# Neighbour masks from ScalarE's bfloat16 copy, and one diagonal add per graph, in a four-layer graph network

## The chip, the cores and the metric

One Trainium2 chip, one of its NeuronCores. The core has TensorE (PE: matmuls and transposes), VectorE (DVE), ScalarE (ACT), GpSimd (POOL) and DMA queues issued by SyncE (SP). The metric is the device time of one execution in microseconds (us); lower is better. Every time here is from runs of the kernel before or from the profile of one such execution.

## What is computed

There are 16 graphs of 1024 nodes with 64 channels, an adjacency matrix of zeros and ones per graph (self-loops included), and four residual layers with normalisation. Layer 0 thins the adjacency and then takes, for each node and channel, a weighted sum of the 25, 50 and 75 % quantiles over the remaining neighbours. Layers 1 to 3 are ordinary graph convolutions with the unthinned adjacency. The change lies in the thinning ("dilation"), whose reference is:

```python
adj_ = jnp.where(eye[None], 1.0, adj)
nb = (adj_ > 0) & (~eye)[None]               # neighbours without the node itself
m = nb.sum(-1)
rank = jnp.cumsum(nb, axis=-1) - 1
skip = jnp.where(m > 10, (m + 1) // 2, 1)
do_dil = (skip > 1) & mask
removed = nb & do_dil[..., None] & ((rank + 1) % skip[..., None] == 0)
rem = removed | jnp.swapaxes(removed, 1, 2)  # removed from either side
return jnp.where(rem, 0.0, adj_)
```

Layer 3 divides by the row sums of the adjacency (plus one), and those row sums are taken in the same pass over the matrix as the dilation.

## The kernel before, in words

**The main loop.** Layer 0 is done by counting. Each graph takes 96 slots (`SLOTS`, L1046), and the loop at L1365 walks 16 x 96 = 1536 slots. In each slot DVE makes one mask (`masks`, L636: tile `mt` from `cc` and `rB`, 128 x 2048) and one product (`products`, L644: tile `pr` from `mt` and `dw`, 128 x 4096). PE multiplies and ACT moves results out of PSUM for several earlier slots (`words` L654, `ranks` L666, `steps` L674) and for the counts of later units (`counts`, L596). A slot has two halves, and a half is called a place.

**Background work.** Between these the loop sets generators, each a piece of other work that is cut into steps by its `yield`s: `sort_pair` with `ranks_of` (L316, L263: the sort of the channel values of two graphs on DVE), `dilate` (L415: the dilation of the next graph), `degrees` (L788: column sums on ACT) and `layers` (L830: the rest of the network for the graph before). `Spread` (L977) decides at every place which generator may take a step. A generator gets a number of steps, a first and a last place, and a step is due when its share of the places has passed (`late`, L1038). A digit that is yielded is a least distance in places to the step before; a `p` marks a step with PE work in the one PSUM bank `ps_l`, of which one is taken per place; `h` holds that bank. `dilate(g + 1)` is given 64 steps over 168 of the graph's 192 places (L1381). The sort is a filler (L1017): it steps where the planner's sum of DVE time (`Ordered.count`, L185) isn't too far ahead of its sum of PE time.

**Order.** While `Ordered.on` holds, each PE, DVE and ACT instruction is linked to the one before it on its engine (`link`, L137), so every engine runs its instructions in just the order in which the Python code issued them. An instruction that waits keeps all behind it on its engine waiting.

**The dilation** works on eight blocks of 128 rows (t = 0 to 7) of the matrix of one graph:

- L422 `block_of` loads a block as two halves `da` of 128 x 512 in float32. There are two such buffers; the loads of block t + 1 are issued right after the readers of block t.
- L435 to L439: for each half, DVE compares (`is_gt` 0) from `da` to the float16 neighbour mask `nb`, and ACT copies `da` to `q`, the block's row of the result tile `vt`, adding up the rows as it goes (`accum_out`). The copy itself is never read.
- L442: DVE clears the diagonal block of `nb` (`offdiag`); L444: DVE scans `nb` to the running count `cum`. `nb` and `cum` are the halves of tile `sc`, of which there is one.
- L451 to L456: POOL works out the row's skip from the last count; L459: ACT overwrites `q` with the distance |cum + bias|, in two halves.
- L464: DVE turns `q` to 1 (removed) or 0.25 (kept). Then two late steps: `edges` (L466) multiplies by `nb`, and `own` (L469) adds 0.25 on the diagonal block, `later` (L205) lets them out one by one after a mask or a product.

When all eight blocks are done, PE transposes pairs of blocks (L484), and DVE combines each with its mirror image (L487, L495), which leaves 1 for an edge that neither side removed.

The dilation of graph 0 runs ahead of the main loop, one step beside each step of the first sort (L1083 to L1100); those of graphs 1 to 15 run beside the main loop of the graph before.

Of the kernel before, what the change touches and what calls it, by code (L numbers as in the profile page):

```python
# [10 lines left out]
F16 = mybir.dt.float16  # L11
BF16 = mybir.dt.bfloat16
# [3 lines left out]
AF = mybir.ActivationFunctionType  # L16
ALU = mybir.AluOpType
AX = mybir.AxisListType

P = 128  # L20
# [22 lines left out]
def gnn_stack(  # L43
# [22 lines left out]
    B, N, C = x.shape  # L66
    H = W1.shape[1]
    L = gW.shape[0]
    T = N // P
    HALF = N // 2  # L70
    V = nc.vector

    const = ctx.enter_context(tc.tile_pool(name="const", bufs=1))
# [27 lines left out]
    ident = const.tile([P, P], F32, name="ident")  # L101
    make_identity(nc, ident)
    ident16 = const.tile([P, P], F16, name="ident16")
    V.tensor_copy(ident16, ident)
    offdiag = const.tile([P, P], F16, name="offdiag")
    V.tensor_scalar(offdiag, ident, -1.0, 1.0, ALU.mult, ALU.add)
    one16 = const.tile([P, 2], F16, name="one16")
    V.memset(one16, 1.0)

# [9 lines left out]
    for i in range(2):  # L119
        t = const.tile([P, N], F16, name=f"prow{i}")  # L120
# [76 lines left out]
    V, A = Ordered(nc.vector, "DVE"), Ordered(nc.scalar, "ACT")  # L197
# [7 lines left out]
    def later(*calls):  # L205

        item = list(calls)
        waiting.append(item)
        return item
# [205 lines left out]
    def dilate(g, found):  # L415

        mk = small.tile([P, T], F32, tag="mk", name="mk")
        V.tensor_copy(mk, mask8[:, g, :])
        den = small.tile([P, 2, T], F32, tag="den", name="den", bufs=3)
        vt = graph.tile([P, T, N], F16, tag="vt", name="vt", bufs=2)  # L420

        def block_of(t):  # L422
            a = []
            for h in range(2):
                a.append(strm.tile([P, HALF], F32, tag="da", name="da", bufs=2))
                nc.sync.dma_start(out=a[h], in_=adj[g, ts(t, P), ts(h, HALF)])
            return a

        a = block_of(0)
        yield  # L430
        for t in range(T):
            sc = dil.tile([P, 2 * N], F16, tag="d", name="sc")
            nb, cum = sc[:, 0:N], sc[:, N : 2 * N]
            q = vt[:, t, :]
            for h in range(2):  # L435
                V.tensor_scalar(nb[:, ts(h, HALF)], a[h], 0.0, None, ALU.is_gt)
                A.activation(
                    q[:, ts(h, HALF)], a[h], AF.Copy, accum_out=den[:, h, t : t + 1]
                )  # L439
            if t + 1 < T:  # L440
                a = block_of(t + 1)
            V.tensor_tensor(nb[:, ts(t, P)], nb[:, ts(t, P)], offdiag, ALU.mult)  # L442

            V.tensor_tensor_scan(cum, nb, nb, 0.0, ALU.add, ALU.max)  # L444
            yield
            m = cum[:, N - 1 : N]


            sk = small.tile([P, 5], F32, tag="sk", name="sk")
            G = nc.gpsimd  # L450
            G.tensor_scalar(sk[:, 0:1], m, 0.5, 0.5, ALU.add, ALU.mult)  # L451
            G.tensor_scalar(sk[:, 0:1], sk[:, 0:1], MAGIC, -MAGIC, ALU.add, ALU.add)
            G.tensor_scalar(sk[:, 1:2], m, T_THRESH, mk[:, t : t + 1], ALU.is_gt, ALU.mult)
            G.tensor_scalar(sk[:, 2:3], sk[:, 0:1], 1.0, sk[:, 1:2], ALU.add, ALU.mult)
            G.tensor_scalar(sk[:, 3:4], sk[:, 2:3], -1.5, 1.5, ALU.mult, ALU.add)
            G.tensor_scalar(sk[:, 4:5], sk[:, 2:3], 0.5, -0.5, ALU.mult, ALU.add)  # L456
            yield "5"

            for h in range(2):  # L459
                A.activation(  # L460
                    q[:, ts(h, HALF)], cum[:, ts(h, HALF)], AF.Abs, bias=sk[:, 3:4]
                )
                yield "2"
            V.tensor_scalar(q, q, sk[:, 4:5], 0.25, ALU.is_equal, ALU.max)  # L464

            def edges(q=q, nb=nb):  # L466
                V.tensor_tensor(q, q, nb, ALU.mult)

            def own(q=q[:, ts(t, P)]):  # L469
                V.scalar_tensor_tensor(q, ident16, 0.25, q, ALU.mult, ALU.add)  # L470

            rest = later(edges, own)
            yield "1"
            finish(rest)
        yield

        tiles = vt.rearrange("p j (t m) -> p j t m", m=P)
        for j in range(T):
            for t0 in range(j + 1, T, 4):
                yield PEV  # L480
                n = min(4, T - t0)
                pq = bank(ps_l, "pq", dt=F16).rearrange("p (i t m) -> p i t m", i=2, m=P)
                for i in range(n):
                    transpose(pq[:, 0, i], tiles[:, t0 + i, j], ident16)  # L484
                    transpose(pq[:, 1, i], tiles[:, j, t0 + i], ident16)
                for i, side in enumerate((tiles[:, j, t0 : t0 + n], tiles[:, t0 : t0 + n, j])):
                    V.scalar_tensor_tensor(  # L487
                        side, pq[:, i, 0:n], 0.25, side, ALU.is_equal, ALU.is_gt
                    )
        yield PEV  # L490
        pq = bank(ps_l, "pq", dt=F16).rearrange("p (t m) -> p t m", m=P)
        for j in range(T):
            transpose(pq[:, j], tiles[:, j, j], ident16)
        side = bass.AP(vt.tensor, vt.offset, [list(vt.ap[0]), [N + P, T], [1, P]])
        V.scalar_tensor_tensor(side, pq, 0.25, side, ALU.is_equal, ALU.is_gt)  # L495
        yield

        rd = dram.tile([S, N], F16, name="rd")
        rn = dram.tile([S, N], F16, name="rn")
        wd = dram.tile([S, N], F16, name="wd", bufs=3)  # L500
        yield PEV
        pm = bank(ps_l, "pm")
        for t in range(T):
            for j in range(T):
                matmul(
                    pm[:, t : t + 1], lhsT=vt[:, j, ts(t, P)], rhs=one16[:, 0:1],
                    start=(j == 0), stop=(j == T - 1), skip_group_check=True,
                )

        def wide_of(i):  # L510
            return by_s[:, i].unsqueeze(1).to_broadcast([P, T, S])

        pos = small.tile([P, T, S], F32, tag="pos", name="pos", bufs=1)
        nb1 = small.tile([P, T], F32, tag="nb1", name="nb1", bufs=1)
        rw = small.tile([P, T, 3 * S], F16, tag="rw", name="rw", bufs=1)
        r, w = rw[:, :, 0:S], rw[:, :, S : 2 * S]
        V.tensor_scalar(nb1, pm[:, 0:T], -1.0, 0.0, ALU.add, ALU.max)
        V.tensor_tensor(pos, nb1.unsqueeze(2).to_broadcast([P, T, S]), wide_of(0), ALU.mult)
        V.tensor_scalar(r, pos, 1023.625, 1024.0, ALU.add, ALU.max)
        V.scalar_tensor_tensor(pos, pos, 1024.0, r, ALU.add, ALU.subtract)  # L520
        V.tensor_tensor(w, pos, wide_of(1), ALU.mult)
        V.tensor_tensor(w, w, wide_of(2), ALU.add)
        V.scalar_tensor_tensor(pos, pos, 0.0, wide_of(3), ALU.is_gt, ALU.mult)
        V.tensor_tensor(r, r, pos, ALU.add)
        V.tensor_scalar(rw[:, :, 2 * S : 3 * S], r, 1.0, None, ALU.add)
        yield "4" + PEN
        pq = bank(ps_l, "pq", dt=F16)
        for t in range(T):
            transpose(pq[0 : 3 * S, ts(t, P)], rw[:, t], ident16)
        sc = dil.tile([P, 2 * N], F16, tag="d", name="sc")  # L530
        A.copy(sc[0 : 3 * S, 0:N], pq[0 : 3 * S])
        nc.sync.dma_start(out=rd, in_=sc[0:S, 0:N])
        nc.sync.dma_start(out=wd, in_=sc[S : 2 * S, 0:N])
        nc.sync.dma_start(out=rn, in_=sc[2 * S : 3 * S, 0:N])
        found.append((vt, rd, rn, wd, den))
# [511 lines left out]
    sorted_, parts, infos = [], [], {}  # L1047
# [189 lines left out]
    for i in range(2):  # L1237
        t = const.tile([P, N], F16, name=f"ranks{i}")
# [125 lines left out]
    pairs_of, background, resident = {}, [], ()  # L1364
    for y in range(n_units * S + S + 2):  # L1365
# [4 lines left out]
        if running and z == 0:  # L1370
            infos[g]["aggd"] = dram.tile([G8, P, HALF], F32, name="aggd")
            deg = small.tile([P, 3, T], F32, tag="deg", name="deg")
            base = 2 * SLOTS * g
            if g == 0 and TURN < B:
                background.append(
                    Spread(
                        sort_of(1, sorted_), 2 * n_sort + 11, 0, base + 2 * SLOTS + ROWS, True
                    )
                )
            if g + 1 < B:  # L1380
                background.append(Spread(dilate(g + 1, parts), 64, base, base + 168))  # L1381
            background.append(
                Spread(degrees(g, deg), 2 * T + 2, base, base + 184)
            )
            infos[g]["deg"] = deg
# [119 lines left out]
```

## Time and profile before

| What | Value |
|---|---|
| median of 3 runs | 8277.14 us (8274.99 to 8284.68) |
| the profiled execution's own time | 8271.02 us |
| its span in the trace | 8269.2 us |
| mean granted TensorE clock | 0.984 |
| first product of the main loop starts | 297.84 us |
| last product starts | 8129.1 us |
| busy DVE, PE, ACT, POOL | 7826.2, 7311.8, 7060.5, 1321.6 us |

All instructions that go through the ordering helper carry the helper's line, L176 (matmuls L156, transposes L152), so groups are told apart by their tiles: `sc<-da` is the compare, `vt<-da` ACT's copy with the row sums, `sc<-sc,offdiag` the clearing of the diagonal, `vt<-vt,sc` the step `edges`, `vt<-ident,vt` the step `own`. A form such as 128x512 f16<-128x512 f32 gives partitions x elements and type of output and input. The start of an instruction and the start of the next one on its engine lie closer together than its listed duration wherever the two may overlap.

### The profile page before, as it was taken

What the parts mean: (1) busy time and instruction counts of PE and PEld (TensorE: products, weight loads), DVE (VectorE), ACT (ScalarE), POOL (GpSimd) and SP (SyncE); (2) the same over time, 40 slices, a digit from 0 to 9 for tenths busy, and PEclk for the clock granted to TensorE, in tenths of its full rate; (3) what the DMA queues carried; (4) which work ended last, traced back from release to release, by engine and by line L of the source; (5) the groups of instructions that cost most, each with busy time, mean ns of one, the idle gap of its engine ahead of it and who ended that gap; (6) DMA issues with size and microseconds to landing.
All of it is one profiled execution on the core that took longest, in us unless ns stands there. A gap on an engine that the chain in (4) does not pass through costs nothing. (4 is left out here: it accounts for less than half of the span.)

```text
span 8269.2 us, 164242 instructions
## 1 busy us (share of the span) xinstructions
PE 7311.8 (88%) x65169; PEld 2994.8 (36%) x65169; DVE 7826.2 (95%) x8924; ACT 7060.5 (85%) x13562; POOL 1321.6 (16%) x942
## 2 busy tenths in 40 slices
PE   0688889999999899898899999999899999999997
PEld 0233333333333333333333333333333333334333
DVE  9899999999999999999999999999999999887874
ACT  1689889888898889989898898988989888899993
POOL 2210202112021110202112021210202112020000
PEclk9999999999999999999999999999999999999999
DMA  3212222232223232232233322233222233222222
GB/s 101 48 42 53 94 88 93 79 101 98 88 86 87 86 104 91 90 93 90 80 99 104 81 93 89 80 100 94 91 94 85 85 97 104 72 89 72 65 88 68
DMA packets 530453, 711.85 MB, mean 86 GB/s; under 512 B 201488, under 2 KB 328848, under 8 KB 529680
## 3 DMA queue, kind: packets, MB, share of 16 engines
q1 hardware_dynamic: 529680, 701.34, 27.3%
q8 instruction: 510, 8.36, 0.4%
q14 instruction: 263, 2.15, 0.1%
HBM read 602.38 MB, written 98.77 MB: 85 GB/s over the span
## 5 line engine op out<-in xcount | busy, mean ns | idle before, releaser
L176 DVE TENSOR_TENSOR pr<-mt,dw 128x4096 f16<-128x4096 f16 x1536 | 3507.8, 2284 | 222.7 <-PE pw L156 166.7
L156 PE MATMUL x<-vt,xw 128*128 128x512 f16 x8192 | 2317.9, 386 | 0.0
L176 DVE TENSOR_TENSOR mt<-cc,rB 128x2048 f16<-128x2048 f16 x1536 | 1864.7, 1214 | 15.4 <-ACT cc L176 15.4
L176 ACT ACTIVATE pv<-pv,col 128x512 f32<-128x512 f32 x1536 | 1077.1, 701 | 0.0
L156 PEld LDWEIGHTS <-xw 128*128 128x128 f16 x8192 | 737.8, 99 | 819.9 <-issue 298.3
L176 ACT ACTIVATE qq<-pw 128x512 f16<-128x512 f32 x1536 | 962.1, 626 | 16.5 <-PE pw L156 15.9
L156 PE MATMUL pv<-mt,txw 128*32 128x512 f16 x12288 | 951.6, 387 | 8.6 <-ACT pv L176 8.6
L176 ACT ACTIVATE val<-pv 128x512 f32<-128x512 f32 x1536 | 948.9, 618 | 9.2 <-PE pv L156 8.9
L156 PE MATMUL pw<-pr,red 128*32 128x512 f16 x12288 | 937.7, 381 | 14.7 <-DVE pr L176 14.7
L176 ACT ACTIVATE pa<-pa,col 128x512 f32<-128x512 f32 x1020 | 712.5, 699 | 224.8 <-PE pa L156 223.2
L176 ACT ACTIVATE dw<-y 128x512 f16<-128x512 f32 x1024 | 636.9, 622 | 261.2 <-PE y L156 238.7
L734 POOL TENSOR_TENSOR rstd<-var,neghalf 128x8 f32<-128x8 f32 x112 | 250.0, 2232 | 3473.9 <-DVE var L176 3473.9
L176 ACT ACTIVATE cc<-x 128x512 f16<-128x512 f32 x1024 | 620.9, 606 | 190.2 <-PE x L156 112.8
L176 ACT ACTIVATE xw<-pa,col 128x512 f16<-128x512 f32 x1020 | 700.8, 687 | 33.0
L176 ACT ACTIVATE dw<-y,col 128x512 f16<-128x512 f32 x1024 | 719.2, 702 | 1.6 <-PE pv L156 1.1
L156 PE MATMUL pw<-ranks,subr 128*32 128x512 f16 x6144 | 603.0, 382 | 66.5 <-ACT xw L176 64.1
L176 ACT ACTIVATE h<-x 128x512 f16<-128x512 f32 x1024 | 640.0, 625 | 1.0 <-PE x L156 1.0
L176 ACT ACTIVATE l<-x 128x512 f16<-128x512 f32 x1024 | 604.0, 590 | 9.4 <-PE x L156 9.2
L156 PE MATMUL pv<-qq,lead 128*32 128x512 f16 x6144 | 603.6, 381 | 0.0
L156 PE MATMUL x<-h,neg 128*128 128x512 f16 x1024 | 393.9, 385 | 225.3 <-ACT h L176 206.4
L156 PEld LDWEIGHTS <-txw 128*32 128x32 f16 x12288 | 186.3, 94 | 1051.0 <-issue 1050.3
L176 DVE TENSOR_TENSOR sr<-sr 128x384 f16<-128x384 f16 (+9 forms) x1328 | 546.4, 441 | 17.7
(226 smaller groups left out, 10547.6 us busy)
## 6 DMA issues: line engine op xcount, KB each, us to landing
a<-adj_dram SPq DMA_DIRECT2D x360, 512.0 KB
a<-adjT_dram SPq DMA_DIRECT2D x240, 512.0 KB
da<-adj_dram SPq DMA_DIRECT2D x256, 256.0 KB
ac<-adjT_dram SPq DMA_DIRECT2D x256, 256.0 KB
aggd<-v SPq DMA_DIRECT2D x128, 256.0 KB
rB<-rn SPq DMA_DIRECT2D x96, 256.0 KB
v<-aggd SPq DMA_DIRECT2D x192, 128.0 KB
w<-wd SPq DMA_DIRECT2D x96, 128.0 KB
```

The costliest lines, as they stand in the source:

```text
L156: link("PE", nc.tensor.matmul(out, **kw))
L176: ins = call(*args, **kw)
L734: nc.gpsimd.tensor_tensor(rstd, var, neghalf, ALU.pow)
```

## The change

The compare no longer reads the float32 block. ACT's copy is written in bfloat16 (the same bytes of `q`, read as another type), and one compare over 1024 elements reads that copy. It is put behind a new `yield "2"`, so at least two places after ACT's instructions were issued. The step `own` is gone; in its place one add per graph, over the eight diagonal blocks together, of a new constant `quarter` (0.25 on the diagonal). The dilation's share of the schedule goes from 64 to 72 steps over the same 168 places. The view `diag`, the same as the former `side`, is made earlier.

```diff
+    quarter = const.tile([P, P], F16, name="quarter")
+    V.tensor_scalar(quarter, ident, 0.25, None, ALU.mult)
...
             q = vt[:, t, :]
+            near = q.bitcast(BF16)
             for h in range(2):
-                V.tensor_scalar(nb[:, ts(h, HALF)], a[h], 0.0, None, ALU.is_gt)
                 A.activation(
-                    q[:, ts(h, HALF)], a[h], AF.Copy, accum_out=den[:, h, t : t + 1]
+                    near[:, ts(h, HALF)], a[h], AF.Copy, accum_out=den[:, h, t : t + 1]
                 )
             if t + 1 < T:
                 a = block_of(t + 1)
+            yield "2"
+            V.tensor_scalar(nb, near, 0.0, None, ALU.is_gt)
             V.tensor_tensor(nb[:, ts(t, P)], nb[:, ts(t, P)], offdiag, ALU.mult)
...
-            def own(q=q[:, ts(t, P)]):
-                V.scalar_tensor_tensor(q, ident16, 0.25, q, ALU.mult, ALU.add)
-
-            rest = later(edges, own)
+            rest = later(edges)
             yield "1"
             finish(rest)
         yield
 
         tiles = vt.rearrange("p j (t m) -> p j t m", m=P)
+        diag = bass.AP(vt.tensor, vt.offset, [list(vt.ap[0]), [N + P, T], [1, P]])
+        V.tensor_tensor(diag, diag, quarter.unsqueeze(1).to_broadcast([P, T, P]), ALU.add)
...
-        side = bass.AP(vt.tensor, vt.offset, [list(vt.ap[0]), [N + P, T], [1, P]])
-        V.scalar_tensor_tensor(side, pq, 0.25, side, ALU.is_equal, ALU.is_gt)
+        V.scalar_tensor_tensor(diag, pq, 0.25, diag, ALU.is_equal, ALU.is_gt)
...
-                background.append(Spread(dilate(g + 1, parts), 64, base, base + 168))
+                background.append(Spread(dilate(g + 1, parts), 72, base, base + 168))
```

## The prediction

> **What bounds the kernel now.** I read the page's busy table first. DVE has the largest share, but an average doesn't say where it counts, so next come the stretches of the span: one of the main loop (3280 to 3480), a leaner one just before it, and the last two graphs.
>
> ```profile
> PE 7311.8 (88%) x65169; PEld 2994.8 (36%) x65169; DVE 7826.2 (95%) x8924; ACT 7060.5 (85%) x13562; POOL 1321.6 (16%) x942
> ```
> ```profile
> core 0: us, PE busy (x) PEld busy (x) DVE busy (x) ACT busy (x) POOL busy (x), PEclk, DMA share, GB/s
> 0.00:150.00 150.00, 9.58 (x76) 6.04 (x77) 143.78 (x300) 36.64 (x93) 44.04 (x98) 1.00 0.31 99
> 150.00:200.00 50.00, 2.55 (x66) 2.19 (x63) 42.78 (x117) 1.20 (x2) 0.00 (x0) 1.00 0.40 111
> ...
> 3160.00:3240.00 80.00, 78.62 (x722) 32.48 (x721) 77.36 (x95) 67.68 (x128) 3.26 (x2) 1.00 0.37 124
> 3280.00:3480.00 200.00, 180.85 (x1615) 72.15 (x1613) 199.42 (x215) 187.07 (x367) 55.16 (x37) 1.00 0.28 93
> ...
> 7200.00:7680.00 480.00, 452.69 (x4118) 184.93 (x4116) 404.40 (x334) 444.77 (x857) 85.62 (x55) 1.00 0.24 79
> ```
>
> In 3280 to 3480 DVE is busy 199.42 of 200 us while PE and ACT have room: DVE's own work is the time there, and that is where the dilation's blocks lie. In 3160 to 3240 PE (78.62 of 80) is as full as DVE (77.36). From 7200 on, where the last dilation runs (its last compare starts at 7454.7), no sort is left, DVE idles 76 of 480 us, and a DVE instruction less is worth nothing. The same stretches for the products alone give the price of a slot: 195 products per 1000 us in the middle, 5.13 us each; 98 in 7200 to 7680, 4.90 us each. So without the sort a graph with a dilation beside it still takes 96 x 4.90 = 470 us against 492. What DVE saves counts fully until a graph has lost some 22 us; then PE and ACT are late next.
>
> The waits of DVE inside the loop agree: between 400 and 8000 us it waits 148.3 us in 133 pieces for PE (`pw`), 125.1 us of it after 7080, where the sort has ended, and never for the dilation's data.
>
> **The compare.** The groups by form give durations, the timeline gives what an instruction really takes of the queue, start to next start:
>
> ```profile
> L176 DVE TENSOR_SCALAR sc<-da 128x512 f16<-128x512 f32 x256 | 96.2, 416 | 0.0
> L176 DVE TENSOR_TENSOR vt<-vt,sc 128x1024 f16<-128x1024 f16 x128 | 87.3, 682 | 0.3
> L176 DVE SCALAR_TENSOR_TENSOR vt<-ident,vt 128x128 f16<-128x128 f16 x128 | 36.0, 281 | 0.0
> L176 DVE SCALAR_TENSOR_TENSOR vt<-pq,vt 128x1024 f16<-128x1024 f16 x16 | 19.5, 1216 | 0.0
> L176 DVE TENSOR_SCALAR sb<-sb 128x1024 f16<-128x1024 f16 x16 | 6.8, 426 | 0.5
> ```
> ```profile
> 3308.92 0.28 DVE L176 SCALAR_TENSOR_TENSOR vt<-ident,vt 128x128 f16<-128x128 f16 x1
> 3309.12 0.75 DVE L176 TENSOR_SCALAR sc<-da 128x512 f16<-128x512 f32 x2
> 3309.79 0.21 DVE L176 TENSOR_TENSOR sc<-sc,offdiag 128x128 f16<-128x128 f16 x1
> 3310.04 2.29 DVE L176 TENSOR_TENSOR_SCAN sc<-sc 128x1024 f16<-128x1024 f16 x1
> ...
> 3341.36 0.69 DVE L176 TENSOR_TENSOR vt<-vt,sc 128x1024 f16<-128x1024 f16 x1
> 3341.97 2.28 DVE L176 TENSOR_TENSOR pr<-mt,dw 128x4096 f16<-128x4096 f16 x1
> 3411.13 0.76 DVE L176 TENSOR_SCALAR sc<-da 128x512 f16<-128x512 f32 x2
> 3411.93 0.23 DVE L176 TENSOR_TENSOR sc<-sc,offdiag 128x128 f16<-128x128 f16 x1
> ```
>
> The pair of compares holds the queue 0.67 us (3309.12 to 3309.79) where the diagonal block lies in the first half, 0.80 (3411.13 to 3411.93) where it lies in the second; mean 0.735. The new compare is one TENSOR_SCALAR of 1024 two-byte elements. The trace has no bfloat16 source, so I bound it: 0.43 from `sb<-sb` (float16, same shape and operation class), 1.22 from the 128x1024 `vt<-pq,vt`, the slowest per element. I take 0.43, the row that differs in nothing but the kind of 16-bit number. The diagonal step depends on it and starts 0.03 after its end, as the scan does here (3309.79 + 0.21 to 3310.04), so 0.46. Saved: 0.735 - 0.46 = 0.275 us per block.
>
> **The diagonal.** `own` has a duration of 0.28 but the next instruction starts 0.20 after it (3308.92 to 3309.12). Eight of these go, 1.60 us per graph. One add of 8 x 128 float16 elements comes. Contiguous, that is `vt<-vt,sc`: 0.69, with the next start after 0.61 (3341.36 to 3341.97). The new one hops between eight blocks and repeats its second operand; `mt<-cc,rB` repeats an operand too and takes 1214 ns for 2048 elements, the same pace. Upper bound 1.22 (`vt<-pq,vt`); I take 0.61.
>
> Per graph: 8 x (0.275 + 0.20) - 0.61 = 3.19 us. Durations alone would say 8 x (752 - 426 + 281) - 682 = 4.17 us, since overlap is counted twice.
>
> Here the Trainium skill speaks for the smaller sum: "Vector Engine (DVE) Microarchitecture Reference", section "Measured stream behaviour on trn2", puts an instruction's fixed cost at about 75 ns once the queue overlaps, so that dropping or merging instructions frees little; "VectorE: DVE Perf Modes" gives about 150 cycles for one by itself, by which the sum would be the larger one. The trace's 0.20 for a 0.28 instruction sides with the first. [...]
>
> **Where it counts.** Dilations of graphs 1 to 14 run beside graphs 0 to 13, where DVE is the bound: 14 x 3.19 = 44.7 us. That of graph 15 runs in the idle of 7200 to 7680: 0. That of graph 0 runs beside the first sort, DVE busy 143.78 of 150: 3.2 us. The setup's extra `quarter` is hidden: the first sort step waits 0.71 us for its data behind the two conversions of `ident`; at worst 4.4 us (`offdiag`, same form, first of its kind).
>
> **What is moved.** The instruction order of the built programs shows eight more steps of graph 0's dilation moving past the end of the sort, among the rank steps, where DVE is idle 7.2 of 50 us (150 to 200) for loads of `m`. Bounds 0 to 7 us; I take 2. In the loop the blocks' compares move from slots 3, 10, 17, 24, 30, 37, 43, 50 to 3, 12, 19, 26, 33, 40, 47, 54, the transposes' combinations from slots 58 to 73 to 62 to 75, the row that hands ranks on from 80 to 76, all inside the 84 at which the next graph takes them; SP's loads of `da` move along, each still a whole block ahead and now freed by ACT alone. The sort, as filler, shifts too: in odd graphs the last 32 slots get 70 instead of 62 sort instructions, the first 24 get 22 instead of 32. The late slots are the lean stretch where PE bounds and DVE had 2.6 us idle in 80. Filling it is a gain of at most that, 7 x 2.6 = 18 us, but crowding slots 24 to 31 (34 instead of 24) could lose as much. I take +4.
>
> **The new wait.** The compare now waits for ACT. Behind it on DVE stand the diagonal step, the 2.29 us scan, and every mask and product; PE waits for those. Before, DVE's compare started between 2.1 us before and 6.0 us after the end of ACT's two copies, median 2.7 over the 128 blocks, -0.6 at worst up to graph 14. Two places are one slot, 5.13 us, so the least margin is about 4.5 us. A row with just this shape exists: `vt<-vt,sk` stands two places behind ACT's second half and waited 0.1 us in all of 128. I price it at 0. If that cover is gone, ACT's two copies with their sum reads take 1.3 us (3305.08 to 3306.40), so 1 us or more per block. ACT's writing of bfloat16 instead of float16 keeps its 0.66 us; between its quickest and slowest 128x512 form (0.59 and 0.70 us) it's off the path, as ACT has 13 us idle in 200. PE's transposes now follow the diagonal add by one to two slots, as they followed `own`; PE's 7.8 us of waiting for `vt` per 1000 us stays.
>
> **Sum:** 44.7 + 3.2 + 2 + 4 = 54 us. The profiled execution took 8271.0 (span 8269.2 plus 1.8), so 8217; the median shown is 6 us above it, so 8277 - 54 = **8223 us**.
>
> **Rivals.**
> - *Larger gain:* the full durations are freed (15 x 4.17 = 63) and the lean stretch fills (+12): 8277 - 75 = 8202. Against it stand the overlapping starts.
> - *Half pace:* a bfloat16 source gets the pace of 16-bit two-operand work, 0.68 as in `vt<-vt,sc`: 15 x 8 x 0.256 = 31 less, 8254. For it: no bfloat16 row.
> - *The planner eats it:* the reshuffled sort leaves PE-bound slots lean and DVE-bound slots crowded, so each graph loses its 3 us again: 8277, within 15. For it: in 3160 to 3240 PE is already full.
> - *Unpacked compare, slower:* the bfloat16 source runs at the pace of `vt<-pq,vt`, 1.22. Place: the 120 compares that count. Price: 1.22 - 0.43 = 0.79 each, 95 us, so 8277 - 54 + 95 = 8318. It turns the sign from a compare of 0.88 us on (54 / 120 = 0.45 above 0.43). Against: the casts in this trace from float32 and int32 to float16 take 0.69 for 1024, below that.
> - *The wait, slower:* ACT lags over 5 us behind; 1 us per block in 14 graphs is 112, 8335; it turns the sign at 0.48 us per block.
>
> **Numbers.** Forecast (8208 to 8240) 0.64; larger gain 0.08; half pace 0.07; planner 0.13; unpacked 0.04; wait 0.04. Changes under 0.2% (16.5 us) are about what can't be told from none. Faster: 0.64 + 0.08 + 0.07 = 0.79; same 0.13; slower 0.08. The range 8200 to 8262 holds the forecast, most of the larger gain, half pace and the planner's better edge, about 0.81.
>
> **What would show it.** In the new profile: a group `sc<-vt` 128x1024 x128 near 426 ns with no idle before it (half pace: 680; unpacked: 1200); no `vt<-ident,vt`; 16 adds `vt<-vt,quarter` near 690; DVE busy down by some 55 us; the middle at 5.10 us per product and 7200 to 7680 unchanged. Idle before `sc<-vt` put down to ACT would prove the wait; more idle of `pr` for PE in mid-loop would prove the planner.

## The result, and the profile after

| Kernel | Median (us) | Lowest to highest | Ratio to before, 95% interval |
|---|---|---|---|
| before | 8277.53 (4 runs) | 8274.99 to 8284.68 | 1 |
| after | 8340.97 (4 runs) | 8332.95 to 8344.41 | 1.0073 [1.0061, 1.0085] |

The changed kernel is 63 us slower; the forecast was 54 us faster, and the time lies outside the range of 8200 to 8262. The profiled execution of after has a span of 8342.3 us (before 8269.2), at a mean granted clock of 0.980 (before 0.984).

First the busy table of after, then the same two stretches as before.

```profile
PE 7344.7 (88%) x65169; PEld 2987.7 (36%) x65169; DVE 7777.7 (93%) x8685; ACT 7083.4 (85%) x13562; POOL 1238.2 (15%) x942
```
```profile
3280.00:3480.00 200.00, 184.22 (x1648) 74.12 (x1645) 195.89 (x197) 190.54 (x372) 46.25 (x32) 0.99 0.24 79
7200.00:7680.00 480.00, 455.25 (x4117) 185.31 (x4118) 399.60 (x318) 444.68 (x855) 79.29 (x55) 1.00 0.25 82
```

DVE has 239 instructions and 48.5 us of work fewer (7826.2 to 7777.7), as was wanted. But the span less DVE's busy time was 443.0 us and is now 564.6: DVE stands idle 121.6 us longer, and 121.6 - 48.5 = 73 is the difference of the two spans. In 3280 to 3480, where DVE had been busy 199.42 of 200 us, it is busy 195.89. The question is what it waits for.

These are the changed instructions in the groups by form of after (count, busy time and mean ns, then idle time just before them):

```profile
L178 DVE TENSOR_SCALAR sc<-vt 128x1024 f16<-128x1024 bf16 x128 | 53.4, 417 | 0.0
L178 DVE TENSOR_TENSOR vt<-vt,quarter 128x1024 f16<-128x1024 f16 x16 | 10.9, 683 | 0.0
```

Both cost what was forecast (426 and 690 ns), and the compare, which now needs ACT's copy, waits 0.0 us. The new wait that a rival feared doesn't exist. The loss is at instructions that the diff doesn't touch. DVE's waits between 400 and 8000 us (total, times, longest), before and after:

```profile
DVE pr L176 <- PE pw L156: 148.3, 133, 2.8
...
DVE x L176 <- POOL rstd L734: 10.3, 10, 1.8
DVE yn L176 <- POOL rstd L734: 5.4, 3, 1.8
```
```profile
DVE pr L178 <- PE pw L158: 152.4, 146, 3.6
DVE yn L178 <- POOL rstd L736: 47.7, 28, 1.8
DVE sr L178 <- DMA rn<-sc: 36.6, 6, 6.4
...
DVE x L178 <- POOL rstd L736: 16.8, 14, 1.8
```

Two waits are new or have grown much. `yn` is the product with the norm's `rstd` in the layers of the graph before; its wait for GpSimd went from 3 times to 28. `sr` is the first rank of a new sort; it stands some 6 us, once in each even graph.

**The first wait in the timeline** (start, duration, engine; in brackets the idle time before), after and then before at the same place:

```profile
2444.26 2.29 DVE L178 TENSOR_TENSOR_SCAN sc<-sc 128x1024 f16<-128x1024 f16 x1
...
2446.70 1.01 POOL L455 TENSOR_SCALAR sk<-sc 128x1 f32<-128x1 f16 x1 [28.63 <-DVE sc L178]
...
2449.78 0.68 DVE L178 TENSOR_REDUCE var<-sq 128x8 f32<-128x512 f32 x1
...
2451.71 2.28 DVE L178 TENSOR_TENSOR pr<-mt,dw 128x4096 f16<-128x4096 f16 x1
2451.80 2.24 POOL L460 TENSOR_SCALAR sk<-sk 128x1 f32<-128x1 f32 x1
...
2454.01 1.65 POOL L736 TENSOR_TENSOR rstd<-var,neghalf 128x8 f32<-128x8 f32 x1
...
2455.69 0.69 DVE L178 TENSOR_TENSOR yn<-pc,rstd 128x512 f32<-128x512 f32 x1 [1.70 <-POOL rstd L736]
```
```profile
2445.56 0.68 DVE L176 TENSOR_REDUCE var<-sq 128x8 f32<-128x512 f32 x1
...
2446.52 2.56 POOL L734 TENSOR_TENSOR rstd<-var,neghalf 128x8 f32<-128x8 f32 x1 [11.84 <-DVE var L176]
...
2447.49 2.29 DVE L176 TENSOR_TENSOR pr<-mt,dw 128x4096 f16<-128x4096 f16 x1
...
2449.70 0.68 DVE L176 TENSOR_TENSOR yn<-pc,rstd 128x512 f32<-128x512 f32 x1
```

In both, the layers' `var` is one product ahead of `yn`, so GpSimd has the time of that product to make `rstd`. Before, GpSimd had idled 11.84 us and began at once; `yn` followed the product without a gap. In after a scan of the dilation ends 3.2 us ahead of the start of `var`, its six `sk` instructions hold GpSimd from 2446.70 to 2454.04, and `rstd` starts at 2454.01 instead of about 2450.7. `yn` comes at 2455.69 after 1.70 us of DVE standing still. The order of the programs says why it is so every time: the scans of a graph moved from slots 30 and 43 to 33 and 47, and `var` of the first two graph layers stands on slots 34 and 47 or 48.

**The second wait**, after and then before: SP issues the sort's eight stores `steps<-sv`, and a few places later DVE makes the first ranks, `sr<-ii`, in the buffer that these stores read (the pool has two, taken in turn).

```profile
2692.96 10.23 SPq L397 DMA_DIRECT2D steps<-sv  x8
...
2700.78 0.68 DVE L178 TENSOR_TENSOR msg<-pa,iv 128x512 f32<-128x512 f32 x1
...
2707.38 0.69 DVE L178 CAST sr<-ii 128x1024 f16<-128x1024 int32 x1 [5.91 <-DMA rn<-sc]
```
```profile
2676.21 10.27 SPq L395 DMA_DIRECT2D steps<-sv  x8
```
```profile
2690.91 0.69 DVE L176 CAST sr<-ii 128x1024 f16<-128x1024 int32 x1 [0.36 <-issue]
```

The copy starts 14.7 us after the first store before (2676.21 to 2690.91) and 14.4 after (2692.96 to 2707.38). So in after the stores set its time, and before, DVE had other work until nearly the same distance: it stood for 0.36 us only (`issue`: the profile shows nothing that it waited for). The stores stood on slot 78 and the copy on 81; now they stand on 80 and 82, a slot of some 5 us closer, and the rest is idle. The release is put down to `rn<-sc`, a row of the dilation that happened to be stored just then (2706.76); a run further down, where that row lies elsewhere, names `steps<-sv`.

Per graph (2 to 12), taken from product to product: even graphs went from 497.2 to 505.1 us (idle 6.4 to 16.4), odd ones from 491.2 to 494.5 (idle 8.0 to 15.2). `yn` takes 3.4 us of idle in each; the rank copy 6.1 and a later `x<-rstd` 1.8 in the even ones.

### The profile page after: what moved, and what is told of

The parts are those of the page before. It is cut to its first block, busy times and chain, and to the rows that moved or that the text cites. A ratio compares the mean times of both kernels' runs of the same rounds, so it can differ in the third digit from the quotient of the medians.

```text
span 8342.3 us, 163984 instructions
## 1 busy us (share of the span) xinstructions
PE 7344.7 (88%) x65169; PEld 2987.7 (36%) x65169; DVE 7777.7 (93%) x8685; ACT 7083.4 (85%) x13562; POOL 1238.2 (15%) x942
## 5 line engine op out<-in xcount | busy, mean ns | idle before, releaser
L455 POOL TENSOR_SCALAR sk<-sc 128x1 f32<-128x1 f16 x128 | 118.2, 923 | 3412.2 <-DVE sc L178 3128.6
```

## The experiments

**Theory:** the work of the change is a gain of about its forecast; its timing is the loss, because steps that were moved now stand directly ahead of others on GpSimd, or closer behind their own stores, and DVE, which keeps its order, waits. **Rivals:** the work itself costs more than its durations say; or the moved sort leaves lean slots to PE (the forecast's "planner").

**The schedule alone.** The old work, with the new place and pace of the compares:

```diff
-                V.tensor_scalar(nb[:, ts(h, HALF)], a[h], 0.0, None, ALU.is_gt)
...
+            yield "2"
+            for h in range(2):
+                V.tensor_scalar(nb[:, ts(h, HALF)], a[h], 0.0, None, ALU.is_gt)
...
-                background.append(Spread(dilate(g + 1, parts), 64, base, base + 168))
+                background.append(Spread(dilate(g + 1, parts), 72, base, base + 168))
```

> Old work in the changed kernel's schedule: the new two-place step and 72 steps, but still two float32 compares per block (after the new step, with the next block's load behind them) and the eight own adds. Output is the reference's. Theory A (the schedule costs: the scans now stand one slot before the layer's variance at slots 33/34 and 47/48, so rstd queues behind the skip's instructions on GpSimd, and the rank copy stands two slots instead of three behind the sort's stores): the changed kernel's 8341 plus the saving that is left out, about 45 to 50, so 8385 to 8395, with some 1.7 us of idle before yn at two places of each graph and 6 us before the rank copy in even graphs. Theory B (the changed instructions themselves cost, in a way the groups don't show): 8277, as before. Theory C (the new planner sums crowd the sort): between, 8300 to 8350, without these two idles.

Measured 8382.35 us, ratio 1.0125 [1.0108, 1.0142]: 106 us slower than before (8276.03 beside it). The waits are those of after:

```profile
DVE yn L176 <- POOL rstd L736: 45.9, 27, 1.8
DVE sr L176 <- DMA rn<-sc: 30.6, 5, 6.3
```

**The work alone.** The new compare and diagonal add, every instruction where it stood before. The edit is against after. Besides leaving out `yield "2"`, ACT's copies of a block (`copy_of`), and with them the next loads, are issued one block step earlier, and the planner is told the old sums of time, so that it places the sort as before (`as_if` adds to its sum of DVE time, and `own` now does only that):

```diff
-            yield "2"
             V.tensor_scalar(nb, near, 0.0, None, ALU.is_gt)
+            Ordered.as_if(75)
...
+            def own():
+                Ordered.as_if(75 + 1.05 * P)
...
+            rest = later(edges, own)
+            if t + 1 < T:
+                copy_of(t + 1, a)
...
-                background.append(Spread(dilate(g + 1, parts), 72, base, base + 168))
+                background.append(Spread(dilate(g + 1, parts), 64, base, base + 168))
```

> All the work of the changed kernel in the order of before: no new step, 64 steps, the planner is told the old sums, and ScalarE's copies of the next block are issued one step earlier, after the block before has its skips, so that the compare finds them done. Output is the reference's. Theory A: 8277 - 45 to 54, so 8223 to 8232, no idle of yn behind rstd beyond that of before and none at the rank copy. Theory B: 8320 or more. Theory C: as A, since the planner's sums are the old ones.

Measured 8233.95 us, ratio 0.9947 [0.9933, 0.9962]: 42 us faster than before, 107 faster than after. `yn<-rstd` is at 5.4 us again and the rank copy's wait gone:

```profile
DVE pr L178 <- PE pw L158: 160.8, 141, 2.9
...
DVE yn L178 <- POOL rstd L752: 5.4, 3, 1.8
DVE sc L178 <- ACT vt L178: 3.7, 7, 2.1
```

So the schedule costs 106 us with the old work and 107 with the new, and the work gains 42: -42 + 106 = +64, and +63 was measured. This kernel is also the fastest of all that ran.

**Only the extra step taken out** of after, with 64 steps in the plan again:

```diff
-            yield "2"
...
-                background.append(Spread(dilate(g + 1, parts), 72, base, base + 168))
+                background.append(Spread(dilate(g + 1, parts), 64, base, base + 168))
```

> The changed kernel without its new step and with 64 steps again: the compare stands right behind ScalarE's copies in the same step. Output is the reference's. Theory A: scans, variances and the rank copy fall on the slots of before, so 8277 - 45 = 8232, plus what the compare now waits for ScalarE (up to 2 us per block where ScalarE was no earlier than VectorE, perhaps 0.5 on the mean: 8232 to 8290). Theory B or C: 8320 or more.

Measured 8241.25 us, ratio 0.9954 [0.9939, 0.9968]. The compare now waits for ACT's copy, but 19 times in 7600 us, 10.5 us in all. The step was put in for this wait, which is about a tenth of what the step cost: after, which differs from this kernel in the step and its places alone, takes 100 us more. This kernel also keeps the planner's new sums of time, so those by themselves cost little: it lies 7 us above the work-alone kernel, about what its waits for ACT add (10.5 us against 3.7).

**The diagonal alone** (before, with `quarter`, one add per graph, and without `own`):

```diff
-            rest = later(edges, own)
+            rest = later(edges)
...
+        V.tensor_tensor(diag, diag, quarter.unsqueeze(1).to_broadcast([P, T, P]), ALU.add)
```

> Before, with only the diagonal's quarters added once per graph. Output is the reference's. Theory A: positions are those of before, and 8 x 0.20 - 0.61 = 1.0 us goes in each of 14 to 15 graphs: 8277 - 14 = 8263. Theory C: 8277 or more.

Measured 8265.58 us, ratio 0.9982 [0.9973, 0.9991]: 10.4 us by the medians, 7 to 22 by the interval, where the forecast's terms give 14 x (8 x 0.20 - 0.61) = 13.9. The trace is finer: graphs 2 to 12 take 5428.5 us from product to product against 5439.7 before, 1.02 less per graph.

**Does such idle time count in full?** Into the work-alone kernel I put idle copies of `var` on GpSimd ahead of `rstd`, in the first two graph layers; nothing else moves:

```diff
+        if name == "yn" and l in (0, 1) and not last_graph:
+            for _ in range(3):
+                again = small.tile([P, T], F32, tag="again", name="again")
+                nc.gpsimd.tensor_scalar(again, var, 1.0, 0.0, ALU.mult, ALU.add)
+                var = again
```

> The old-order kernel of the fourth run (8234), with three idle copies of the variance on GpSimd ahead of rstd in the first two of the three graph layers, all but the last graph: they stand for the skip's instructions. Output is the reference's. Theory A (VectorE, in order, stands while GpSimd is late): each copy 0.3 to 2 us, so yn waits 1 to 4 us at two places in 15 graphs: 8264 to 8350, all of it as idle of yn released by rstd. Rival (such waits are taken back within the slack of PE and ScalarE): 8234 to 8245 in spite of the idle.

Measured 8289.51 us, ratio 1.0013 [1.0004, 1.0022], so 55.5 over the kernel that it is built on (53 if each is taken against the runs of before beside it).

```profile
DVE yn L178 <- POOL rstd L757: 64.3, 31, 2.6
```

`yn` waits 59 us more (64.3 against 5.4), `x` 2 less; the spans of the two profiled executions differ by 53.0. These waits of some 2 us on GpSimd, an engine that is 17% busy here, cost nearly their whole length: DVE is the bound and keeps its order.

**The rank copy one slot nearer its stores**, in the work-alone kernel:

```diff
-            yield "4"
+            yield "2"
             yield from ranks_of(rows, False)
```

> The old-order kernel of the fourth run (8234) with one digit altered: the rank copy keeps two places instead of four to the sort's stores, so it falls on slot 80, two slots behind slot 78, as in the changed kernel; scans and variances stay. Output is the reference's. Theory A (the copy starts 5.7 us after the last store was issued, whatever its slot, and VectorE stands until then): 5 to 6 us of idle before it in each of seven even graphs: 8234 + 35 to 42, so 8269 to 8276. Rival (the idle is taken back in the lean slots behind it): 8234 to 8245.

Measured 8265.37 us, ratio 0.9986 [0.9977, 0.9996]: 31 us over its base (29 if each is taken against the runs of before beside it), for 26 us more of `sr` and 11 more of `x`. Here no `rn<-sc` is near, and the wait is put down to the stores; the copy starts 15.3 us after the first store (2662.64 to 2677.96).

```profile
DVE sr L178 <- DMA steps<-sv: 26.9, 6, 5.0
DVE x L178 <- POOL rstd L752: 21.2, 16, 1.8
```

**Mending after instead.** Four attempts to take the waits away while keeping the new schedule. First the rank copy one slot later (`yield "4"` to `yield "6"`):

> The changed kernel with one digit altered: the rank copy keeps a distance of six places instead of four to the sort's stores (slot 83 instead of 82, with everything else on its slot). Output is the reference's. Theory A, first half (the rank copy waits for the stores' transfers): the idle of 6 us before it goes in the seven even graphs, and with it most of the 7.8 us of extra idle in slots 80 to 87: 8341 - 37 to 47, so 8294 to 8304; the idles of yn stay. Rival (the late slots are lean whatever the copy does): 8335 to 8341, with the idle moved to another instruction.

Measured 8324.32 us, ratio 1.005 [1.0033, 1.0067]: 17 us under after, less than half of what was expected. The copy itself still stands 1.5 to 2.1 us in each of six even graphs, 11 us in all under four DMAs' names, again 14.3 to 15.1 us after its first store. `sr` also waits 15.5 us for the next thing in the sort, its loads `m<-swaps`, and in slots 88 to 95 idle went from 0.6 to 3.1 us per even graph. `yn` keeps its 47.7 us, as it should.

Then two places instead of one between `rstd` and its product:

```diff
-        yield KEEP
+        yield KEEP + "2"
...
-                return place >= self.held + (2 if "p" in self.next else 1)
+                return place >= self.held + (2 if "p" in self.next or "2" in self.next else 1)
```

> The changed kernel with two places instead of one between rstd on GpSimd and the product that uses it. That also shifts the sort's end, so that the rank copy stands three slots behind the stores again (78 and 81). Output is the reference's. Theory A: both idles go, 8341 - 45 - 42 = 8254, perhaps 10 more for what else is moved. Rival (GpSimd's lateness is a symptom of lean slots): 8300 or more.

Measured 8279.01 us, ratio 0.9998 [0.9989, 1.0007]: 62 under after, but 25 over the expectation. `yn` fell to 8.5 us, and the stores and the copy moved to slots 78 and 81 by themselves, so that wait fell from 36.6 to 10.7 us (in the list it is `sr` with `least<-back`: the same copy, 14.8 to 16.1 us after its first store). Others came up:

```profile
DVE pr L178 <- PE pw L158: 153.5, 123, 3.4
DVE pr L178 <- ACT pa L178: 33.4, 18, 2.3
DVE m L178 <- DMA sv<-xT_dram: 31.6, 6, 5.7
...
DVE sr L178 <- DMA least<-back: 10.7, 6, 2.6
DVE yn L178 <- POOL rstd L736: 8.5, 21, 1.8
```

`m<-sv` is the sort's first compare. In this kernel its last loads leave SP at 3146.80 and the compare stands until 3152.05. I put a distance of four places between these loads and the compare (`yield "4"` ahead of the sort's loop, and one step more in its plan):

> The sixth run's kernel (8279; the changed work and schedule, two places for rstd), with one more step of four places between the sort's loads and its first compare, where that run and the seventh stood 5 us each time. Output is the reference's. Theory A: this idle goes in seven odd graphs, 8279 - 36 = 8243; the shift by one step may open a smaller gap elsewhere (up to 8255). Rival (the late slots of odd graphs are bound by TensorE anyway): 8270 to 8279.

Measured 8280.23 us, ratio 1.0003 [0.9993, 1.0012]: no gain. The wait for the loads is gone, and the same 5.2 us per odd graph stand in the same slots 72 to 79 in front of `pr`, for PE (153.5 to 179.7). There TensorE is next behind the loads. What was expected of taking this wait away failed, and the rival given with it held.

Last, after with 77 steps instead of 72, which puts the scans on slots 3, 11, 18, 25, 31, 38, 45 and 51, clear of `var`:

> The changed kernel with 77 steps instead of 72, nothing else: scans on 31 and 45 instead of 33 and 47, variances on 34 and 47, stores and rank copy on 78 and 81. Output is the reference's. Theory A: both idles go without any of the work altered: 8232 to 8250. Rival (the extra step itself or the later compare costs): 8300 or more.

Measured 8320.4 us, ratio 1.0049 [1.0034, 1.0064], a clear miss. `yn` fell to 3.6 us, but other waits grew; what stands ahead of `x` was not traced back:

```profile
DVE x L178 <- POOL rstd L736: 33.2, 28, 1.8
DVE m L178 <- DMA sv<-xT_dram: 27.3, 6, 5.6
...
DVE sr L178 <- DMA m<-swaps: 11.2, 11, 1.6
```

**What stays open.** The cost of the schedule is shown as a whole (106, 107 and 100 us by three pairs of kernels). Of its parts, 42 us of `yn` and some 41 of `sr` and `x` are seen in the trace and, in like doses, priced by the two runs above (55.5 us for 57 of idle, 31 for 37): 42 x 55.5 / 57 + 41 x 31 / 37, about 75. The trace of the schedule-alone kernel places a little more: over its whole span DVE stands idle 105.6 us longer than before, about 83 of them at `yn`, `sr` and `x`, and 13 at `pr` for PE (166.7 to 179.9). What is left lies in small waits that no run separates. Nor was it separated what holds the kernels with two places some 45 us above the work-alone kernel, or whether the granted clock has a part: it was 0.980 to 0.982 in the runs of after and 0.979 to 0.981 with the schedule alone, against 0.982 to 0.985 in those of before. The stretch from the start of the last product took 148.5 us in the profiled execution of after against 140.1 before, but 142.8 in the schedule-alone kernel, so I don't count it as an effect of the schedule.

## Why the prediction was wrong, point by point

- **The failed step** is "What is moved". It listed the new slots of the scans, named that they are "all inside the 84 at which the next graph takes them", checked ACT's margin and PE's lean slots, and took +4 us of gain. The slots of DVE's steps were right. A deadline was the wrong test for them: the steps were held against the reader of their results, and not against the other work on GpSimd that they now stand ahead of; and the sort, of which it says that it "shifts too", was not held against the 14 us that its stores need before the rank copy. The price of this step was 106 us of loss (schedule alone), 110 away from what was taken. Both collisions could be read before: the order of the two programs shows `var` on slots 34 and 47 beside the scans' new 33 and 47, and DVE's 0.36 us ahead of the rank copy was in the trace.
- **The compare:** right. 417 ns for 426, with a bfloat16 source; the half-pace and the unpacked rival fall. The Trainium skill's "Vector Engine (DVE) Microarchitecture Reference", section "Performance modes", asks for two-byte types, besides conditions on the layout, for the fourfold pace of an operation with one source such as TENSOR_SCALAR, not for a particular two-byte type. The 417 ns from bfloat16 beside 426 from float16 agree.
- **The diagonal:** right. 683 ns an add; 1.02 us per graph in the trace for 0.99 forecast, 10.4 us by the medians for 13.9.
- **Fixed cost:** the sum by starts was the right one: the diagonal alone gains 1.02 per graph, against 0.99 by starts and 8 x 0.281 - 0.683 = 1.57 by durations. The same reference's section "Measured stream behaviour on trn2", with its fixed cost of about 75 ns per instruction after queue overlap, is on that side.
- **Where it counts:** the term was 3.19 us per graph; the work-alone kernel shows 30.1 us over 11 graphs (5439.7 to 5409.6), 2.74 each. Mis-sized by a seventh, and in the compare's term: 2.74 - 1.02 = 1.72 per graph for 8 x 0.275 = 2.20. Graph 0's terms (3.2 + 2) were too large as well: the main loop starts 0.8 us earlier in after, 2.5 with the work alone. The sum of the work's terms (44.7 + 3.2 + 2 = 50) measured 42.
- **Last dilation worth nothing:** right; graph 14 took 473.6 us before, 473.3 with the work alone.
- **The new wait:** right that it costs 0; the compare waits 0.0 us in after. The rival "the wait, slower" names 8335, close to the measured 8341, and is wrong all the same, and its number near by chance: it needed idle before `sc<-vt`, and there is none.
- **The planner eats it:** nearest in kind, since the loss comes through the order that the planner makes. But its mechanism (PE-bound lean slots) and its price (0 net, within 15) aren't what was found.
- **The range** failed because no case in it let the schedule itself lose more than the work gains. 18 us either way were put on it, from the 2.6 us that DVE stands idle in the lean slots.

## What to carry to other kernels

A background step that moves has to be held against every in-order queue that it passes, not against its deadline alone: list what now stands within its duration ahead of it and behind it on GpSimd and on the DMA issuer, do the same for what shifts along with it, and look for the bound engine behind that. Small gaps ahead of a DMA's release in the trace before (0.36 us here) are distances that hold by accident; a wait on a nearly idle engine can cost close to its full length when the bound engine keeps its order (53 to 55.5 us for 57 here). When a change alters both the work and its timing, build each alone: here -42 and +106 told at once where to look.

## What the runs showed of the hardware that had not been expected

- A compare from bfloat16 to a float16 mask runs at the pace of float16: 417 ns for 128x1024, next start 0.45 us after its own (2443.55 to 2444.00).
- GpSimd's six instructions on one column (128x1) hold it 7.3 us (2446.70 to 2454.04), beside DVE's large two-byte operations; single ones of the six vary from 0.23 to 2.24 us.
- Eight stores `steps<-sv` take 10.2 to 11.0 us to issue, and the copy into a buffer that they read starts 14.4 to 15.3 us after the first of them, in the timelines of before, after and the kernel with the rank copy one slot nearer; in the last two it stood waiting for them.
- The releaser that a wait is put down to can be wrong for DMAs: 36.6 us were listed under `rn<-sc`, and where that row lay elsewhere, the same wait stood under `steps<-sv`, or, with the copy one slot later, under four other names.
